# Four buffers instead of two for the sums of overflow rows and of lists in a graph kernel

## The chip, the cores and the metric

One core of one Trainium2 chip. The metric is the device time of one execution in microseconds; the lower the better. The kernel before has a median of 2090.91 us over three runs.

## The reference, cut to what matters

One layer of a graph network: 6250 nodes of 128 features, 200000 edges. Each edge takes the transformed features of its `dst` node, multiplies them by a filter made from 20 edge features, and the products are added up by the edge's `src` node.

```python
h = relu(layernorm(x))                                   # 6250 x 128
xw = h @ W_in
W = (softplus(edge_attr @ W_f1 + b_f1) - log 2) @ W_f2 + b_f2   # 200000 x 128
W = W * edge_weight
m = xw[dst] * W                                          # gather by dst (sorted)
out = segment_sum(m, src, 6250)                          # scatter-add by src (random)
return x + (softplus(out @ W_o1 + b_o1) - log 2) @ W_o2 + b_o2
```

The edges are sorted by `dst`, so a gather reads from a narrow window of rows. The `src` indices are in random order: the segment sum is the costly part.

## The kernel before, in words

The edges are cut into quads of 512 (four chunks of 128); there are 391. A hand-written software pipeline runs one loop iteration `i` per quad. In each iteration the matmuls of several quads at different stages are issued, and at named points (`"D0"`, `"A0"`, `"DM"`, `"PE2"`, `"A2"`, `"D2"`, `"S"` and so on) the loop runs whatever functions were hooked there for this iteration. The order of instructions on each engine is the order of these calls; nothing is rescheduled.

The common part of each quad: PE makes the filter's first product `z` (L313); ACT takes exp and ln of it (tile `a`, L318 and L323); PE gathers node rows by a one-hot matmul (`xg`, L497) and makes the filter `W` (L494, L505); ACT scales the gathered rows into `xc` (L510, four instructions); DVE multiplies `W` by `xc` (L520). PSUM is split into two tags of four banks: "A" (`z`, `xg`, `W`) and "B" (nearly everything else, among it `osum`, `lsum`, `un`, `pq`, `po`).

What becomes of the messages depends on the quad:

- Plain quads (the first and last ones): duplicates within a chunk are summed by a matmul, ACT copies the sums to a tile `s` and makes the indices `ji` (L563), and four scatters follow.
- List quads (192 of them, 768 scatters): the messages in tile `s` are scattered straight from L520's result, with indices prepared ahead (`lji`). Rows that occur twice in a chunk go to a side list in memory; each of 12 such lists is later loaded, summed by a matmul (`lsum`, L469 and L470) and scattered.
- Sorted quads (168 of them): the messages are split into three bf16 parts (tile `pt`, L676, with an extension copied by ACT at L682), permuted into groups of node ranges by matmuls (`pq`, L687), copied to `mst` by ACT (L693), and every eight quads summed straight into node columns by 96 matmuls of a unit (`un`, L781), which DVE adds into `accT` (L792). A unit needs all four "B" banks. Rows that find no slot overflow: they go through `po` (L702 to L704) into `mo` (L710), and every two quads the overflow rows are summed over equal nodes (`osum`, L741) and scattered.

Every scatter is an indirect DMA with accumulation that POOL issues (L582), into one of four accumulators in memory. There are 987: 768 from lists' quads, 123 from plain quads, 96 of the sums of overflow rows and lists (84 + 12).

The part that the change touches is the end of the last two branches. For a pair of sorted quads, or a list, in this order:

1. PE makes the sum in a "B" bank (`over_sum`, or `l_sum`), hooked at `"PE2"`.
2. In the next iteration, at `"A0"`, ACT copies it to the SBUF tile `os` (`over_copy` L746, `l_copy` L475). This frees the PSUM bank. Both write the same tag "os".
3. At `"DM"`, after the iteration's four `xc`, DVE computes the row that the sum goes to (`over_ji` L751, `l_ji` L481, tile `ojd`, three buffers).
4. At `"A2"` ACT turns it into an integer (`over_int` L755, tile `oji`, two buffers).
5. One iteration later, at `"S"`, POOL scatters `os` by `oji` (`over_scatter`).

A tile's buffers are reused in turn. The write to a buffer waits until the instruction that last read it is done; for `os` and `oji` this is the scatter, and "done" means that its data have landed in memory. ACT's instructions run in the order of issue, so a waiting one holds up all behind it. ACT's order in an iteration is: exp and ln of the quad, copies of plain quads, `"A0"` (among it L746, L475, the `mst` and `mo` copies), `ji`, `"A1"`, the four `xc`, then `"A2"` (L755, then L682).

```python
for c in range(4):
    nc.tensor.matmul(W[:, c, :], st[q]["a"][:, c * P:(c + 1) * P], w2, start=False, stop=(c == 3))
...
at(k, "PE2", over_sum, q)
at(k + 1, "A0", over_copy, q)
at(k + 1, "DM", over_ji, q)
at(k + 1, "A2", over_int, q)
at(k + 2, "S", over_scatter, q)
```

After the last scatter the accumulators are loaded, added, transposed and sent through the closing two matrices (L1362 to L1409).

Of the kernel before, what the change touches and what calls it, by code (L numbers as in the profile page):

```python
# [7 lines left out]
F32 = mybir.dt.float32  # L8
# [12 lines left out]
P = 128  # L21
# [33 lines left out]
def tile_gnn(ctx: ExitStack, tc: tile.TileContext, x, fB, cT, srcT, srcr, dstr, win_, wf1, wf2, bias, bo1c, wo1,  # L55
# [53 lines left out]
    sp_ = edge.enter_context(tc.tile_pool(name="sp", bufs=4))  # L109
# [361 lines left out]
        mp["L", j]["sum"] = t  # L471

    def l_copy(j):
        s = sp_.tile([P, 132], F32, tag="os", name="os", bufs=2)
        nc.scalar.copy(s[:, :P + 1], mp["L", j].pop("sum")[:, :P + 1])  # L475
        mp["L", j]["os"] = s

# [264 lines left out]
        mp[q]["sum"] = t  # L742

    def over_copy(q):
        s = sp_.tile([P, 132], F32, tag="os", name="os", bufs=2)
        nc.scalar.copy(s[:, :P + 4], mp[q].pop("sum")[:, :P + 4])  # L746
        mp[q]["os"] = s

# [87 lines left out]
    with tc.manual_schedule():  # L836
# [289 lines left out]
        for w in range((LE - LB) // SW):  # L1126
# [26 lines left out]
            at(k - 1, "L", l_load, w)  # L1153
            at(k, "PE2", l_sum, w)
            at(k + 1, "A0", l_copy, w)
            at(k + 1, "DM", l_ji, w)
            at(k + 1, "A2", over_int, ("L", w))
# [5 lines left out]
        for q in mpq:  # L1163
# [19 lines left out]
            if mpi[q] % 2 or q == mpq[-1]:  # L1183
                at(q + 5, "DM", over_idx, q)
                at(q + 6, "A0", over_dg, q)
                k = clear(q + 6, units)
                at(k, "PE2", over_row, q)
                at(k + 1, "D0", over_eq, q)
                k = clear(q + 8, units)
# [5 lines that stand above are left out]
# [85 lines left out]
    with tc.For_i(0, trips, 1) as ci:  # L1280
# [55 lines left out]
        s = wk.tile([P, P], F32, bufs=1, tag="dg", name="fs")  # L1336
# [259 lines left out]
```

## Time and profile before

| what | us |
|---|---|
| median of three runs (2089.85 to 2092.94) | 2090.91 |
| the profiled execution | 2069.4 |
| its span | 2067.6 |
| PE busy | 1854.7 |
| DVE busy | 1657.1 |
| POOL busy | 1631.5 |
| ACT busy | 1490.1 |

How to read the lines that follow: an engine's row in a timeline begins with the start and the duration in us, then engine, line, operation, output and inputs; in square brackets stands how long the engine was idle just before and what released it. In a view of waits a row says who waited for whom, the sum in us, how many times, and the longest one. In a row of groups, "x768 | 1237.3, 1611 | 266.9" is the count, busy us, mean ns of one, and the idle time just before them. POOL's span of a scatter ends when it has issued it; the data land later.

### The profile page before, as it was taken

The numbers are of one execution on the slowest core, as the hardware profiler recorded it, in microseconds if no ns is written. First come the engines' busy times: TensorE is split into PE (matmuls) and PEld (weight loads), VectorE is DVE, ScalarE is ACT, GpSimd is POOL, SyncE is SP. The second block draws the span as 40 slices with busy tenths as digits, with TensorE's granted clock in tenths as the row PEclk, the third lists the DMA queues.
The fourth block names the chain that finished last, engine by engine and source line by source line (L and its number), as shares of the span: only waits on it lengthen the run. The fifth ranks groups of instructions, "written<-read, shape, count | busy, mean of one in ns | idle before, by whom it ended". The sixth has DMA issues, their size and how long they took to land. (4 is left out here: it accounts for less than half of the span.)

```text
span 2067.6 us, 57535 instructions
## 1 busy us (share of the span) xinstructions
PE 1854.7 (90%) x20381; PEld 1285.7 (62%) x20381; DVE 1657.1 (80%) x4448; ACT 1490.1 (72%) x4083; POOL 1631.5 (79%) x1040
## 2 busy tenths in 40 slices
PE   3489997999999999999999999999999999999956
PEld 2356664666666666666666666666666666677734
DVE  3578896898987888988988978979889787787735
ACT  3368775777776788777778777777778678888714
POOL 3578888888877788887878878888888888888774
PEclk9689998999999999999999999999999999999978
DMA  7887766767766776766667666676676676667648
GB/s 240 227 211 150 125 124 109 128 112 135 130 124 106 126 133 117 136 124 122 121 133 123 122 123 117 118 129 107 129 128 116 112 126 111 110 120 131 129 46 242
DMA packets 381187, 272.56 MB, mean 132 GB/s; under 512 B 97727, under 2 KB 341354, under 8 KB 380898
## 3 DMA queue, kind: packets, MB, share of 16 engines
q0 software_dynamic: 143728, 71.30, 34.9%
q1 hardware_dynamic: 236882, 197.50, 33.8%
q8 instruction: 161, 2.64, 0.5%
q14 instruction: 128, 1.05, 0.2%
q10 hardware_dynamic: 288, 0.07, 0.0%
HBM read 154.45 MB, written 114.24 MB: 130 GB/s over the span
## 5 line engine op out<-in xcount | busy, mean ns | idle before, releaser
L582 POOL DMA_INDIRECT acc<-s,lji x768 | 1237.3, 1611 | 266.9 <-issue 184.6
L687 PE MATMUL pq<-pt,pm 128*128 128x387 bf16 x2688 | 527.9, 339 | 27.0 <-DVE pt L676 10.7
L510 ACT ACTIVATE xc<-xg,cb 128x128 f32<-128x128 f32 x1564 | 446.4, 371 | 121.0 <-PE xg L497 113.8
L505 PE MATMUL W<-w,a 128*128 128x128 f32 x3128 | 464.1, 293 | 0.0
L505 PEld LDWEIGHTS W<-w,a 128*128 128x128 f32 x3128 | 388.7, 196 | 42.0 <-issue 2.6
L781 PE MATMUL un<-so,mst 32*128 32x392 bf16 x8064 | 378.3, 331 | 31.9 <-ACT os L746 19.3
L693 ACT CAST mst<-pq 128x387 bf16<-128x387 f32 x672 | 303.1, 481 | 132.6 <-PE pq L687 130.0
L687 PEld LDWEIGHTS <-pm 128*128 128x128 bf16 x2688 | 259.4, 99 | 211.4 <-issue 16.7
L781 PEld LDWEIGHTS <-mst 32*128 32x128 bf16 x8064 | 228.4, 94 | 175.0 <-issue 70.0
L323 ACT ACTIVATE a<-a,con 128x512 f32<-128x512 f32 x391 | 282.3, 722 | 12.7
L582 POOL DMA_INDIRECT acc<-s,ji x123 | 197.0, 1602 | 82.8 <-issue 25.9
L318 ACT ACTIVATE a<-z 128x512 f32<-128x512 f32 x391 | 237.4, 607 | 33.2 <-PE z L313 17.4
L676 DVE TENSOR_TENSOR pt<-pt 128x512 f32<-128x512 f32 x336 | 231.8, 690 | 5.8
L662 DVE TENSOR_SCALAR pm<-iot,pos 128x576 bf16<-128x576 f16 x672 | 221.4, 390 | 0.0
L520 DVE TENSOR_TENSOR s<-W,xc 128x512 f32<-128x512 f32 x192 | 131.9, 687 | 92.9 <-ACT xc L510 86.0
L792 DVE TENSOR_TENSOR accT<-un,accT 128x392 f32<-128x392 f32 x320 | 158.5, 558 | 58.4 <-PE un L781 58.2
L766 DVE TENSOR_SCALAR so<-iot,mst 128x392 bf16<-128x392 f16 x672 | 191.2, 344 | 5.5 <-PE un L781 5.4
L582 POOL DMA_INDIRECT acc<-os,oji x96 | 155.6, 1621 | 31.1 <-issue 16.2
L497 PE MATMUL xg<-wn,oh 63*128 63x128 bf16 x1564 | 157.2, 222 | 14.5 <-ACT xc L510 8.1
L313 PE MATMUL z<-ft,ws 123*128 123x512 bf16 x391 | 151.6, 388 | 16.1 <-POOL b2rep L927 9.3
L494 PE MATMUL W<-b2rep,onesb 64*128 64x512 bf16 x391 | 153.8, 393 | 0.0
L520 DVE TENSOR_TENSOR pt<-W,xc 128x512 f32<-128x512 f32 x168 | 115.2, 686 | 34.9 <-ACT xc L510 29.4
(209 smaller groups left out, 2431.1 us busy)
## 6 DMA issues: line engine op xcount, KB each, us to landing
rb<-reld SPq DMA_DIRECT2D x391, 64.0 KB
fsd<-f SPq DMA_DIRECT2D x49, 480.0 KB
ft<-fsd SPq DMA_DIRECT2D x195, 120.0 KB
sb<-src SPq DMA_DIRECT2D x169, 128.0 KB
fb<-in_fB_dram SPq DMA_DIRECT2D x49, 320.0 KB
ft<-fsd SPq DMA_DIRECT2D x195, 80.0 KB
wn<-tab SPq DMA_DIRECT2D x782, 15.8 KB
acc<-s,lji POOLq DMA_INDIRECT x768
```

The source lines that it names most:

```text
L318: nc.scalar.activation(a, st[q]["z"], AF.Exp)
L323: nc.scalar.activation(a, a, AF.Ln, bias=half, scale=0.5)
L505: nc.tensor.matmul(W[:, c, :], st[q]["a"][:, c * P:(c + 1) * P], w2, start=False, stop=(c == 3))
L510: nc.scalar.mul(xc[:, c, :], st[q]["xg"][:, c, :], late["c", q // CQ][:, 4 * (q % CQ) + c:4 * (q % CQ) + c + 1])
L520: nc.vector.tensor_tensor(m[:, :, :P], st[q]["W"], st[q]["xc"], op=ALU.mult)
L582: nc.gpsimd.indirect_dma_start(out=accs[k][:rows, :], out_offset=bass.IndirectOffsetOnAxis(ap=ji, axis=0), in_=s, in_offset=None, compute_ ...
L662: nc.vector.tensor_scalar(pm[:, c], iot[:, :SLOTS], rk[r]["pos"][:, 4 * j + c:4 * j + c + 1], None, op0=ALU.is_equal)
L676: nc.vector.tensor_tensor(pt[:, :, k * P:(k + 1) * P], a, high(a), op=ALU.subtract)
L687: nc.tensor.matmul(t[:, :PW], mp[q]["pm"][:, c, s * P:(s + 1) * P], high(mp[q]["pt"][:, c:c + 1, :PW])[:, 0], start=(c == 0), stop=(c == 3))
L693: nc.scalar.copy(mp[q]["ms", s][:, :PW], mp[q].pop(("q", s))[:, :PW])
L766: nc.vector.tensor_scalar(so, iotw[:, :GN], w[:, 3 * P // 2:3 * P // 2 + 1], None, op0=ALU.is_equal)
L781: nc.tensor.matmul(ts[g][:, :GN], mp[q]["ms", s][v, k * P:(k + 1) * P], mp[q]["oh"][v], start=(q == qs[0] and k == 0), stop=(q == qs[-1] a ...
```

## The change

The tag "os" gets four buffers instead of two, at both places that write it. Nothing else is edited; `oji` keeps two buffers and `ojd` three. Each `os` buffer is 132 float32 per partition.

```diff
     def l_copy(j):
-        s = sp_.tile([P, 132], F32, tag="os", name="os", bufs=2)
+        s = sp_.tile([P, 132], F32, tag="os", name="os", bufs=4)
         nc.scalar.copy(s[:, :P + 1], mp["L", j].pop("sum")[:, :P + 1])
...
     def over_copy(q):
-        s = sp_.tile([P, 132], F32, tag="os", name="os", bufs=2)
+        s = sp_.tile([P, 132], F32, tag="os", name="os", bufs=4)
         nc.scalar.copy(s[:, :P + 4], mp[q].pop("sum")[:, :P + 4])
         mp[q]["os"] = s
```

## The prediction

> **What bounds the kernel now.** I read the page first (the parts on busy time, slices, chain of waits and costliest groups), then the views of the tile os, of its two source lines, of the waits of POOL by window, and the timelines of ACT, PE and POOL around the places that these gave.
>
> ```profile
> span 2067.6 us, 57535 instructions
> ...
> PE 1854.7 (90%) x20381; PEld 1285.7 (62%) x20381; DVE 1657.1 (80%) x4448; ACT 1490.1 (72%) x4083; POOL 1631.5 (79%) x1040
> ...
> POOL 3578888888877788887878878888888888888774
> ...
> PE 33%; DVE 7%; ACT 3%; DMA 2%; POOL 2%; issue 1%; SPq 1%; DVEq 0%; POOLq 0%; ACTq 0%
> ...
> L582 POOL DMA_INDIRECT acc<-s,lji x768 | 1237.3, 1611 | 266.9 <-issue 184.6
> ```
>
> Two engines are nearly full. PE is busy 90% and leads the chain of waits. POOL looks free at 79%, but its scatters stand 0.30 us apart even where nothing is waited for (the "issue" rows below), so one scatter occupies about 1.61 + 0.30 = 1.91 us, and the 987 of them (768 + 123 + 96) 1885 us of the 2067.6. The kernel ends with POOL: its last scatters run without a gap, and the closing sums wait for the last one.
>
> ```profile
> 1954.26 1.54 POOL L582 DMA_INDIRECT acc<-s,ji  x1 [2.43 <-ACT ji L563]
> ...
> 2006.32 1.54 POOL L582 DMA_INDIRECT acc<-os,oji  x1 [0.30 <-issue]
> ```
>
> So a gain anywhere counts only if it makes POOL's last scatter earlier, that is, if it removes a POOL pause longer than 0.30 us. Those pauses, from the first stall named below to the second, and from the second to the last scatter:
>
> ```profile
> POOL acc L582 <- issue: 148.5, 487, 0.3
> POOL acc L582 <- DVE s L520: 24.4, 18, 3.0
> ...
> POOL acc L582 <- DVE bn L186: 10.9, 7, 2.2
> ```
>
> ```profile
> POOL acc L582 <- ACT ji L563: 5.8, 5, 2.4
> ...
> POOL acc L582 <- ACT a L318: 1.6, 3, 1.0
> POOL acc L582 <- DMA acc<-os,oji: 1.4, 1, 1.4
> ```
>
> Less 0.30 for each, the first stretch has 24.4 - 5.4 + 10.9 - 2.1 = 27.8 us in which POOL had caught up with the engines that feed it; the second has 4.3 + 0.7 = 5.0 us of that kind, and 1.1 us more that a DMA caused.
>
> **What the change touches.** The view of the tile os:
>
> ```profile
> L582 POOL DMA_INDIRECT acc<-os,oji x96: 1541/1542/2527, 185.5 to 2006.3; - x96
> L746 ACT COPY os<-osum x84: 247/248/269, 154.1 to 1981.2; 128x132 f32<-128x132 f32 x84
> ...
> L475 ACT COPY os<-lsum x12: 247/249/270, 337.7 to 1885.1; 128x129 f32<-128x129 f32 x12
> ...
>   DMA acc<-os,oji: 18.2, 2
> ...
>   PE un L781: 19.3, 4
> ```
>
> With two buffers, copy k must wait until the scatter of copy k-2 has landed. Of the 93 copies that carry such a wait (below), two had to stand: 18.2 us together. In both, PE's unit matmuls (un, L781) stood still behind the copy for the PSUM bank it empties.
>
> **The change part by part.** No instruction is added, dropped or reordered on any engine in the listing of both programs; only ACT's waits differ. All 81 + 12 = 93 DMA waits leave L746 and L475, and 93 appear at L755, the oji write, which keeps its two buffers and whose buffer is read by the same scatter k-2. So the wait isn't removed: it moves down ACT's queue, past the os copy, any mst and mo copies (L693, L710) and the four xc (L510) of the same iteration. Behind it still stand the next pt (L682) and the next exp and ln (L318, L323). SP and POOL are passed by nothing; DMA issues are untouched.
>
> First place, the copy held up near 350 us (ACT, then PE, then the scatter that it waited for on POOL):
>
> ```profile
> 361.25 0.27 ACT L746 COPY os<-osum 128x132 f32<-128x132 f32 x1 [13.77 <-DMA acc<-os,oji]
> ...
> 362.42 0.32 ACT L755 ACTIVATE oji<-ojd,con 128x1 int32<-128x1 f32 x1
> ...
> 368.53 1.14 ACT L510 ACTIVATE xc<-xg,cb 128x128 f32<-128x128 f32 x4 [3.97 <-PE xg L497]
> ```
>
> ```profile
> 361.56 6.58 PE L781 MATMUL un<-so,mst 32*128 32x392 bf16 x93 [14.18 <-ACT os L746]
> ...
> 368.08 0.39 PE L497 MATMUL xg<-wn,oh 63*128 63x128 bf16 x4
> ```
>
> ```profile
> 357.94 1.54 POOL L582 DMA_INDIRECT acc<-os,oji  x1 [0.30 <-issue]
> ```
>
> After the change the copy runs at 361.25 - 13.77 = 347.5, then xc; ACT stands at L755 instead, until the same 361.25. PE does its un (and the next W and xg) inside that wait. From 361.25 on ACT runs the work that began at 362.42, so 1.17 us earlier: it reached the end of it at 368.53 - 3.97 = 364.56, now at 363.4, and there xg is ready. The next xc starts at 363.4 instead of 368.53: a lead of 5.1 us for what feeds POOL. Bounds: nothing (if PE is late anyway) and 13.8 (the whole wait). I take 5.1, since its rows are read directly.
>
> One row speaks against it: after 14 us of idling the 93 un took 6.58 us, where others take 4.09 for 96 (the chain of waits), so 3.96 for 93: a slow restart that costs 2.6 us.
>
> ```profile
> 1657.25 4.09 PE un L781 x96
> ```
>
> The Trainium skill (TensorE: Matmul & The Clock Gate, What's actually happening) says the PE clock falls to half after an idle window of about 3.4 us and returns after as much work. By that rule PE, which would still idle some 7 us ahead of 361.3, restarts slow after the change as well; if PE rather than ACT then decides, the first lead is 2.6 us less and the sum 2064.1 us instead of 2061.5.
>
> The sum stays with 5.1: ACT's own work between 361.3 and 363.4 covers most of a slow restart of PE, and the lead of PE is larger than that of ACT (its pq and xg have no un ahead of them).
>
> Second place (ACT, PE, POOL):
>
> ```profile
> 1633.71 0.27 ACT L746 COPY os<-osum 128x132 f32<-128x132 f32 x1 [4.43 <-DMA acc<-os,oji]
> ...
> 1635.51 0.32 ACT L755 ACTIVATE oji<-ojd,con 128x1 int32<-128x1 f32 x1
> ...
> 1637.87 0.73 ACT L280 CAST f<-fr 128x640 bf16<-128x640 f32 x1 [0.70 <-DVE fr L276]
> 1641.34 1.14 ACT L510 ACTIVATE xc<-xg,cb 128x128 f32<-128x128 f32 x4 [2.75 <-PE xg L497]
> ```
>
> ```profile
> 1634.03 6.92 PE L781 MATMUL un<-so,mst 32*128 32x392 bf16 x93 [4.52 <-ACT os L746]
> ```
>
> Here un fits wholly into the wait: from 1629.5 at the other units' rate it ends at 1633.5, and PE never idles. ACT goes on at 1633.71 with what began at 1635.51 (1.80 earlier), reaches L280 at 1637.17 - 1.80 = 1635.4, and xc at about 1636.0 instead of 1641.34: 5.3 us.
>
> What becomes of each lead? While POOL is behind, it can't use it; it gets it back at the next pauses. The first lead meets 27.8 us of pauses, so it arrives in full. The second meets only 5.0 us, all near the end. On the way it makes POOL later relative to ACT, so a copy with a small margin may now wait. The smallest margin behind 1634 us:
>
> ```profile
> 1756.57 1.54 POOL L582 DMA_INDIRECT acc<-os,oji  x1 [0.30 <-issue]
> ```
>
> ```profile
> 1761.74 0.25 ACT L746 COPY os<-osum 128x132 f32<-128x132 f32 x1
> ...
> 1762.89 0.32 ACT L755 ACTIVATE oji<-ojd,con 128x1 int32<-128x1 f32 x1
> ```
>
> ```profile
> 1762.04 4.14 PE un L781 x93
> ```
>
> The scatter ends at 1758.11 and, by the two stalls (361.25 - 359.48 and 1633.71 - 1631.13), lands 1.8 to 2.6 us later. L755 comes 2.2 to 3.0 us after that. With ACT 5.3 us earlier it would wait 2.3 to 3.1 us. Un's 4.14 us run meanwhile and hide it; without that cover the second lead loses it. Bounds of the second lead at the end: 0 and 5.0. I take 3.5.
>
> Cost of the wait itself. An instruction that waits for two engines gets a separate semaphore instruction:
>
> ```profile
> L746 ACTq EVENT_SEMAPHORE  x41: 17/17/17, 192.5 to 1951.4; - x41
> ...
> L475 ACTq EVENT_SEMAPHORE  x9: 17/17/17, 337.1 to 1750.3; - x9
> ```
>
> ```profile
>   DVE ojd L751: 43.0, 36
> ```
>
> Before there were 50, 17 ns each; now all 93 oji writes wait for DMA and DVE and need one, so 43 more: 0.7 us. The Trainium skill says the same of such instructions (Perfetto Trace Analysis, Identifying Dependency Chains: instructions waiting on several engines may have EventSemaphore instructions inserted ahead of them). ACT is idle 28% of the span, so this is an upper end; nothing is the lower. The larger os tile only shifts addresses in SBUF, at no cost.
>
> Sum: 2069.4 (the profiled execution: 2067.6 of span and 1.8 around it) - 5.1 - 3.5 + 0.7 = 2061.5 us, a ratio of 0.9962. The runs shown have a median of 2090.91, 21.5 us above the profiled execution; nothing in the trace shows why. On their scale the ratio gives 2083 us.
>
> **The rivals.** (A) The wait only changes its place. ACT stands at L755 as long as at L746, everything of the next iteration is behind it, and POOL's own load decides. For it: the DMA that ends the wait is the same, and POOL paces the stretch from 1634 us to the end. Against it: un's work moves ahead of the wait, and POOL has 27.8 us of pauses later. Time: from nothing to one shrunken lead, 5.1 - 2.6 = 2.5 us; 2088.4 to 2091.
>
> (B) Slower: the waits at L755 break ACT's pipelining. Where L755 didn't wait for DVE (93 - 36 = 57 places) it starts ahead of the end of the last xc, as the two timelines show (361.41 + 1.15 against 362.42 at the first place: 0.14 us). If the separate semaphore instruction ends this overlap at the 57 and ACT decides there, that is 57 x 0.14 = 8.0, with the 0.7 some 8.7 us; with the leads lost as in A, about 2099.6 us. It decides once its price exceeds the leads that arrive. Against it: L746 has carried such instructions 41 times and is not seen to start later than without; ACT has idle time in nearly every iteration.
>
> ```profile
> 361.41 1.15 ACT L510 ACTIVATE xc<-xg,cb 128x128 f32<-128x128 f32 x4
> ```
>
> (C) More gain. Margins at several list copies are small, and unprofiled executions are 21.5 us longer; if part of that is further stalls of this kind, twice the forecast's gain, 2 x 7.9, is there: 2075 us. Nothing in the one trace shows it.
>
> **How the numbers follow.** Forecast (both leads arrive in the main) 0.49; A 0.31; B 0.13; C 0.07. 0.2% is 4.2 us, about what a measurement of this kernel can tell from no change. Faster: forecast and C, 0.56; within: A, 0.31; slower: B, 0.13. The predicted time is the forecast's 2083. The range reaches down to C (2075, and 2 us of run spread: 2073) and up past all of A to 2094, which leaves most of B out.
>
> **What would show it.** Right: no idle time ahead of L746 and L475 by DMA; one wait of 12 to 13 us at L755 near 350 us and one of about 2 us near 1632; no un waiting for os; un at about 4.1 us in both places; the next xc some 5 us earlier against the same scatter; POOL's pauses between 362 and 640 us shorter by 5 us in sum. Wrong: POOL's pauses unchanged in sum, new stalls at L755 at other places that stop PE, or L755 starting later after the last xc at most of its places.

## The result, and the profile after

The changed kernel takes 2081.45 us (median of 17 runs) beside 2088.73 us before: a ratio of 0.9967, 95% interval 0.9955 to 0.9979, so some 7 us or 0.33% faster. Two later measurements of the same two kernels, below, gave 0.9966 and 0.9971. The forecast was 0.9962.

The page of the changed kernel's profiled execution:

```profile
span 2077.4 us, 57578 instructions
...
PE 1862.5 (90%) x20381; PEld 1288.0 (62%) x20381; DVE 1659.4 (80%) x4448; ACT 1482.8 (71%) x4083; POOL 1643.9 (79%) x1040
...
PE 31%; DVE 6%; ACT 3%; DMA 3%; issue 2%; POOL 2%; SPq 1%; DVEq 0%; POOLq 0%; ACTq 0%
...
L582 POOL DMA_INDIRECT acc<-s,lji x768 | 1245.7, 1622 | 266.6 <-issue 180.3
```

This one execution is longer than the profiled one of before (2077.4 against 2067.6 us), though the kernel is faster. Single executions of the kernel before lie between 2071 and 2092 us on one chip, so two spans say nothing of a gain of 7 us; that is left to the timed ratios. What a trace does show is where the wait stands and what gets ahead of it. The view of the tile os after the change:

```profile
L582 POOL DMA_INDIRECT acc<-os,oji x96: 1541/1542/2397, 186.8 to 2015.6; - x96
L746 ACT COPY os<-osum x84: 247/248/270, 156.6 to 1991.5; 128x132 f32<-128x132 f32 x84
...
  PE un L781: 2.0, 6
```

The entry "DMA acc<-os,oji: 18.2, 2" is gone from the list of what os waits for, and un waits for os 2.0 us instead of 19.3. The wait itself isn't gone. The view of L755:

```profile
L755 ACT ACTIVATE oji<-ojd,con x96: 294/308/327, 160.3 to 1992.0; 128x1 int32<-128x1 f32 x96
L755 ACTq EVENT_SEMAPHORE  x93: 17/17/17, 197.6 to 1963.1; - x93
...
  DVE ojd L751: 35.3, 27
  DMA acc<-os,oji: 20.0, 3
```

ACT stands 20.0 us at three places, about as long as the 18.2 us before, only further down its queue. The first place, in the timelines of ACT and of PE:

```profile
352.65 0.25 ACT L746 COPY os<-osum 128x132 f32<-128x132 f32 x1
352.80 1.14 ACT L510 ACTIVATE xc<-xg,cb 128x128 f32<-128x128 f32 x4
368.41 0.29 ACT L755 ACTIVATE oji<-ojd,con 128x1 int32<-128x1 f32 x1 [14.47 <-DMA acc<-os,oji]
...
370.28 1.12 ACT L510 ACTIVATE xc<-xg,cb 128x128 f32<-128x128 f32 x4
```

```profile
352.95 4.13 PE L781 MATMUL un<-so,mst 32*128 32x392 bf16 x93 [0.29 <-ACT os L746]
357.02 0.39 PE L494 MATMUL W<-b2rep,onesb 64*128 64x512 bf16 x1
...
368.85 2.74 PE L687 MATMUL pq<-pt,pm 128*128 128x387 bf16 x8 [10.04 <-ACT pt L682]
```

The copy and xc are done at once, un runs in the wait, and so do the next W and xg. Then PE idles 10 us for pt, which ACT makes behind the wait. Before, the next xc came 368.53 - 361.25 = 7.3 us after the wait ended; now it comes 370.28 - 368.41 = 1.9 us after. That is a lead of 5.4 us, where 5.1 was forecast.

The second place, and the one that had the smallest margin (ACT):

```profile
1646.45 0.29 ACT L755 ACTIVATE oji<-ojd,con 128x1 int32<-128x1 f32 x1 [2.81 <-DMA acc<-os,oji]
...
1648.60 1.13 ACT L510 ACTIVATE xc<-xg,cb 128x128 f32<-128x128 f32 x4
```

```profile
1774.06 0.29 ACT L755 ACTIVATE oji<-ojd,con 128x1 int32<-128x1 f32 x1 [2.70 <-DMA acc<-os,oji]
```

At the second, the next xc follows the end of the wait by 2.2 us instead of 1641.34 - 1633.71 = 7.6: 5.4 us. At the third a new wait of 2.70 us appears, where 2.3 to 3.1 was worked out.

### The profile page after: what moved, and what is told of

It reads as the page before. It is cut to its first block, busy times and chain, and to the rows that moved or that the text cites. A ratio compares the mean times of both kernels' runs of the same rounds, so it can differ in the third digit from the quotient of the medians.

```text
span 2077.4 us, 57578 instructions
## 1 busy us (share of the span) xinstructions
PE 1862.5 (90%) x20381; PEld 1288.0 (62%) x20381; DVE 1659.4 (80%) x4448; ACT 1482.8 (71%) x4083; POOL 1643.9 (79%) x1040
## 5 line engine op out<-in xcount | busy, mean ns | idle before, releaser
L323 ACT ACTIVATE a<-a,con 128x512 f32<-128x512 f32 x391 | 282.3, 722 | 12.7
L582 POOL DMA_INDIRECT acc<-s,ji x123 | 200.2, 1628 | 80.4 <-issue 26.4
L318 ACT ACTIVATE a<-z 128x512 f32<-128x512 f32 x391 | 238.3, 610 | 26.8 <-PE z L313 17.2
L520 DVE TENSOR_TENSOR s<-W,xc 128x512 f32<-128x512 f32 x192 | 131.9, 687 | 85.9 <-ACT xc L510 52.0
L520 DVE TENSOR_TENSOR pt<-W,xc 128x512 f32<-128x512 f32 x168 | 115.2, 686 | 47.9 <-ACT xc L510 29.5
```

The lines of the kernel that those rows point to most:

```text
L318: nc.scalar.activation(a, st[q]["z"], AF.Exp)
L323: nc.scalar.activation(a, a, AF.Ln, bias=half, scale=0.5)
L520: nc.vector.tensor_tensor(m[:, :, :P], st[q]["W"], st[q]["xc"], op=ALU.mult)
L582: nc.gpsimd.indirect_dma_start(out=accs[k][:rows, :], out_offset=bass.IndirectOffsetOnAxis(ap=ji, axis=0), in_=s, in_offset=None, compute_ ...
```

## The experiments

All ratios are to the kernel before, timed on the same chip beside each run. A ratio compares all runs and can differ by 0.1% from the quotient of the two medians. The rows stand for 12 runs each, those from both deeper to lists apart for 6, the last one for 2. The chips differ by more than the change brings: the kernel before has medians of 2071.1, 2082.5 and 2082.9 us on the three chips of these runs. The lead theory says: the gain is the work of ACT and PE that gets ahead of the wait. Its rivals: the move alone does nothing and POOL's load decides; or any change of buffers does this.

| kernel | os / oji buffers | median us, before us | ratio, 95% interval |
|---|---|---|---|
| before, again | 2 / 2 | 2082.7, 2082.5 | 1.0006, 0.9987 to 1.0026 |
| before, a third time | 2 / 2 | 2084.3, 2082.9 | 1.0006, 0.9990 to 1.0022 |
| only oji deeper | 2 / 4 | 2082.5, 2082.5 | 1.0006, 0.9990 to 1.0022 |
| oji write later | 2 / 2 | 2071.0, 2071.1 | 1.0007, 0.9990 to 1.0023 |
| changed, again | 4 / 2 | 2073.4, 2082.5 | 0.9966, 0.9950 to 0.9983 |
| changed, a third time | 4 / 2 | 2076.2, 2082.9 | 0.9971, 0.9955 to 0.9987 |
| changed, oji write later | 4 / 2 | 2063.9, 2071.1 | 0.9965, 0.9947 to 0.9984 |
| both deeper | 4 / 4 | 2060.4, 2082.5 | 0.9904, 0.9883 to 0.9925 |
| both three | 3 / 3 | 2063.3, 2082.9 | 0.9910, 0.9888 to 0.9932 |
| both four, oji write later | 4 / 4 | 2063.7, 2082.9 | 0.9911, 0.9893 to 0.9928 |
| lists apart | 2 + 2 / 2 + 2 | 2051.3, 2071.1 | 0.9912, 0.9889 to 0.9934 |
| no scatter of sums | 4 / 2 | 2040.0, 2071.1 | 0.9857, 0.9819 to 0.9895 |

**The two kernels again.**

> The kernel before once more, on the chip of the next three. All theories: a ratio of 1.000 within 0.002. Lead theory (what counts is how much of ACT's and PE's work gets ahead of the wait): again a wait of 12 to 15 us ahead of L746 near 350 us with un (L781) idle for as long, and the next xc (L510) 7 to 8 us after the wait ends.

> The changed kernel once more. Lead theory: a ratio of 0.9955 to 0.998; the wait of 12 to 15 us now ahead of L755, the next xc about 2 us after it ends, un idle for under 3 us in sum because of os. Rival (only the place of the wait changes, POOL's load decides): the same wait, but a ratio within 0.002 of 1.

> The kernel before a third time, for one more trace and timing on this chip: ratio 0.998 to 1.002; a wait of 12 to 15 us ahead of L746 near 350 us and one of 1 to 5 us near 1640 us.

> The changed kernel a third time: ratio 0.995 to 0.998. Counted from the iteration ahead of the first stall, the tenth iteration behind it starts 4 to 5 us sooner than in the kernel before; single executions scatter by more than that at the end.

All four came as the lead theory has it: 12.6 and 13.7 us ahead of L746 in the traces of the kernel before, 12.1 and 12.7 us ahead of L755 in those of the changed one. Two sizes were a little off: in the first repeat of the kernel before the next xc comes 6.5 us after the wait, not 7 to 8, and in the last pair the 67th iteration of the table below starts 5.5 us sooner, not 4 to 5 (4.7 as the mean over all traces). Only the second, small stall is unsteady: 1.8 and 4.4 us before, none at that place in these two after. The rival that puts the ratio within 0.002 of 1 falls.

**Only oji deeper.**

```diff
-        ji = sp_.tile([P, 1], I32, tag="oji", name="oji", bufs=2)
+        ji = sp_.tile([P, 1], I32, tag="oji", name="oji", bufs=4)
```

> os keeps two buffers, oji gets four. Lead theory: the wait stays ahead of L746, no work gets ahead of it, so a ratio of 0.998 to 1.002. Rival (any change of buffers or of their places in SBUF moves the time as the change did): about 0.9967.

1.0006. In its view of os the wait is still there:

```profile
  PE un L781: 19.1, 7
  ACT os L746: 17.4, 2
```

(the list of who waited: un for os, and the copy itself for the scatter that reads os). So it isn't more buffers of any kind, or other places of them, that bring the gain.

**Both deeper.** The changed kernel with the same edit of oji.

> Four buffers for os and for oji, so the wait is gone and not only moved. Lead theory: at the first place ACT gains the whole 13.8 us instead of some 5.4, and POOL has 27.8 us of later pauses to take it in: 6 to 9 us below the changed kernel, a ratio to before of 0.992 to 0.994. Rival (POOL's backlog decides: with the wait gone the tile s, which has four buffers, holds DVE up instead): the same ratio as the changed kernel, 0.996 to 0.998, with new waits of 5 us and more at L520 on scatters.

0.9904: 20 us below before and 13 below the changed kernel, clear of the rival's bounds, and more than the 6 to 9 us expected of the lead theory, which had counted the first place alone. The whole of the two waits came back (18.2 us in the profile of before; 12.6 + 1.8 to 13.7 + 4.4 in the repeats). ACT at the first place:

```profile
351.43 0.25 ACT L746 COPY os<-osum 128x132 f32<-128x132 f32 x1
351.58 1.14 ACT L510 ACTIVATE xc<-xg,cb 128x128 f32<-128x128 f32 x4
352.59 0.32 ACT L755 ACTIVATE oji<-ojd,con 128x1 int32<-128x1 f32 x1
...
356.72 1.14 ACT L510 ACTIVATE xc<-xg,cb 128x128 f32<-128x128 f32 x4 [1.99 <-PE xg L497]
```

No wait at either line; the next xc comes 5.3 us after the copy, where it took 17.6 in the changed kernel. The granted TensorE clock stays at 1.00 from 340 to 380 us, so that PE's slow restart is gone as well. The tile s did not take the wait over: L520 waits for scatters 1.9 us in all.

**Lists apart.** os and oji keep two buffers; the sums of lists get tags of their own, two buffers each.

```diff
     def l_copy(j):
-        s = sp_.tile([P, 132], F32, tag="os", name="os", bufs=2)
+        s = sp_.tile([P, 132], F32, tag="los", name="os", bufs=2)
...
     def over_int(q):
-        ji = sp_.tile([P, 1], I32, tag="oji", name="oji", bufs=2)
+        t_ = "loji" if isinstance(q, tuple) else "oji"
+        ji = sp_.tile([P, 1], I32, tag=t_, name="oji", bufs=2)
```

> os and oji keep two buffers for overflow sums, and the lists' sums get two of their own for each. Lead theory, with the stalls put down to the lists (a list's sum between two overflow sums takes a buffer out of turn): an overflow copy then waits for a scatter one turn earlier, no wait is left at L746, L475 or L755, and the ratio is that of four buffers for both, 0.988 to 0.993. Rival (two buffers are too few whatever the lists do): waits of 5 us and more stay and the ratio is 0.995 to 1.001.

0.9912 and no wait at any of the three lines. This names the cause of the stalls. Overflow copies come some 20 us apart, a scatter waits its turn on POOL for up to 35 us, and two buffers just suffice, until a list's sum comes in between and takes one. At both stalls of the kernel before the order was overflow sum, list, overflow sum, and the third had to wait for the first's scatter. The copies ahead of the first stall and of the second:

```profile
322.81 0.25 ACT L746 COPY os<-osum 128x132 f32<-128x132 f32 x1
...
337.69 0.25 ACT L475 COPY os<-lsum 128x129 f32<-128x129 f32 x1
```

```profile
1605.64 0.25 ACT L746 COPY os<-osum 128x132 f32<-128x132 f32 x1
...
1616.16 0.27 ACT L475 COPY os<-lsum 128x129 f32<-128x129 f32 x1 [0.29 <-PE lsum L470]
```

Behind the first place DVE now waits a little for s instead:

```profile
DVE s L520 <- DMA acc<-s,lji: 8.0, 4, 3.0
```

**Both three.**

> Three buffers for os and for oji. In the traces of before, the scatter three back had ended 14 us ahead of the copy at the first stall, so three are enough: no wait at L746, L475 or L755, ratio as with four of each, 0.988 to 0.993. Rival (depth itself brings more): between the changed kernel and four of each, 0.993 to 0.997.

0.9910 and no wait at the three lines: three are enough, as the scatter three back was always done.

**The oji write one iteration later.** In the changed kernel, in the one before, and with four buffers for both:

```diff
-            at(k + 1, "A2", over_int, ("L", w))
+            at(k + 2, "A2", over_int, ("L", w))
...
-                at(k + 1, "A2", over_int, q)
+                at(k + 2, "A2", over_int, q)
```

> The changed kernel (os four, oji two) with the oji write one iteration later, still ahead of its scatter. Lead theory: pt, exp, ln and the next four xc get ahead of the wait too, about 3 to 5 us of ACT's work more than in the changed kernel, so 3 to 6 us below it: a ratio to before of 0.993 to 0.9955. Rival (moving a wait that isn't removed brings a fixed amount, whatever stands ahead of it): 0.996 to 0.998 as the changed kernel.

> The kernel before (two buffers for both) with the oji write one iteration later. It has what later_os4 does besides moving the wait: ACT no longer idles ahead of L755 for DVE's ojd (about 43 us in sum). Lead theory: that idle time isn't on the path that sets the end, and the wait stays at L746: 0.997 to 1.002. Rival: ACT's idle time ahead of L755 counts, then several us are gained, 0.993 to 0.997.

> Four buffers for both and the oji write one iteration later. Lead theory: no wait is left to be moved, and ACT's idle time for ojd was off the path, so the same as four of each: 0.988 to 0.993. Rival (that idle time counts once the stalls are gone): below 0.988.

The two controls came as the lead theory had them, 1.0007 and 0.9911: ACT's idle time ahead of L755 for DVE's ojd (43.0 us before, none here) was worth nothing. The first missed. 0.9965 is the changed kernel's ratio, not 0.9930 to 0.9955. The trace shows why the expectation was too large:

```profile
352.74 1.14 ACT L510 ACTIVATE xc<-xg,cb 128x128 f32<-128x128 f32 x4 [1.52 <-PE xg L497]
363.62 0.29 ACT L755 ACTIVATE oji<-ojd,con 128x1 int32<-128x1 f32 x1 [9.75 <-DMA acc<-os,oji]
363.82 0.58 ACT L318 ACTIVATE a<-z 128x512 f32<-128x512 f32 x1
```

The second xc does get ahead of the wait, but in the changed kernel all of pt, exp, ln and xc took only 371.28 - 368.41 = 2.9 us after it (the next exp began at 371.28). Counted from the anchor of the table below, the 67th iteration starts at 53.6, 1.4 us sooner than in the changed kernel, less than 0.1%, and the interval is 0.18% wide on each side. The direction agrees with the lead theory; the timing can't tell it from the rival, which stays open.

**No scatter of sums.** The scatter of the 96 sums is left out, the rest of the changed kernel stays.

> The changed kernel without the 96 scatters of overflow and list sums (these sums are left out of the output). If POOL's load sets the end, 96 x 1.91 = 183 us of it are gone and the time falls until PE sets it: over 40 us below the changed kernel. If PE sets the end and POOL has room, it falls by under 20 us.

Between the two: about 23 us below the changed kernel (0.9857 against 0.9966 to 0.9971), and only some 10 below the kernels without the wait, for 183 us less of POOL's work. With two runs either difference is uncertain by some 8 us. POOL's waits in it:

```profile
POOL acc L582 <- issue: 207.1, 676, 0.6
POOL acc L582 <- DVE s L520: 126.9, 51, 7.6
POOL acc L582 <- ACT ji L563: 46.6, 10, 18.7
POOL acc L582 <- DVE bn L186: 34.8, 15, 5.3
```

So most of what is taken from POOL turns into waiting for the engines that feed it. They in turn wait for PE: DVE's `s` for ACT's xc (87.3 us), ACT's xc for PE's xg (105.0 us), and PE is busy 91%. PE's side sets the pace, with POOL close behind.

**The traces laid side by side.** The starts of the exp (L318) of each iteration, read from ACT's timelines and counted from the 58th, the last but two ahead of the first stall:

```
iteration   four traces with the stall at L746     three of the changed kernel   both 4, both 3, both 4 later, apart
67th        59.7  58.5  60.6  60.0                 56.0  54.5  54.5              44.4  44.2  45.2  43.4
319th       1283.3 1292.6 1291.6 1293.6            1288.1 1292.6 1288.4          1281.5 1279.1 1281.4 1265.5
325th       1318.5 1324.1 1325.6 1328.2            1319.9 1322.2 1318.6          1310.1 1307.1 1310.4 1294.3
391st       1627.4 1635.4 1636.6 1640.9            1631.5 1633.2 1629.6          1621.2 1618.2 1622.2 1603.4
```

(The four are the three of the kernel before and the one with only oji deeper; the kernel before with the later oji write, which stalls at L746 too, has 59.3 at the 67th. Lists apart ran on the chip of 2071.1 us, so its later rows don't compare with the others.) At the 67th the groups are well apart: 59.7 on average, 55.0 and 44.3. The first lead is 4.7 us, and 15.4 with the wait gone; that is more than the wait itself (12.6 to 13.8 us), as PE's slow restart behind it is gone too. From the 319th to the 325th, across the second place, the groups take 33.8, 30.5 and 28.6 us: leads of 3.3 and 5.2. At both places together that makes 8.0 us for the changed kernel and 20.6 for the wait-free ones, beside timed gains of some 7 and of 18 to 20 us. In between single executions drift by 10 us, so that no trace follows a lead to the end; only the wait-free kernels remain visibly ahead.

## Why the prediction was right

- **The wait moves, it doesn't go.** Right: 20.0 us in three places at L755, none at L746 and L475; un waits 2.0 instead of 19.3 us. The controls show that it is this: deeper oji alone does nothing, deeper both brings 0.9904. The first wait was to be 12 to 13 us; it is 14.5, 12.1 and 12.7 in the three traces.
- **The first lead, 5.1 us.** 5.4 in the two rows that the forecast named, 4.7 as the mean of the traces.
- **PE's slow restart.** After 10.04 us of idling the eight pq took 2.74 us, where eight take 1.40 in the many rows of the chain of waits of before: 1.3 us of loss, not 2.6, and ACT's exp, ln and xc covered it. One of these rows:

```profile
1088.26 1.40 PE pq L687 x8
```

  The granted TensorE clock shows the restart itself. It is 0.50 from 349.5 to 366.6 us in the kernel before and from 361.3 to 371.6 in the changed one. At the second place it is 0.50 from 1632.9 to 1639.7 before, where un took 6.92 us, and 1.00 after the change: there the slow restart is gone, as the forecast's "PE never idles" had it. By the Trainium skill (TensorE: Matmul & The Clock Gate, What's actually happening) an idle window of about 3.4 us halves the clock until PE has been busy for such a window. The traces agree: the three slow stretches last 17.07, 10.24 and 6.83 us, which is 5, 3 and 2 times 3.41. At the first place un, which no longer idles first, took 4.13 us instead of 6.58.
- **The second lead, 5.3 us, of which 3.5 was to arrive.** 5.4 by the rows of the two profiled executions, 3.3 as the mean over traces, since the wait that it comes from is between 1.8 and 4.4 us. The new wait at the place of the smallest margin was foreseen with its size (2.70 us); in another execution it is 3.7 us, in a third it isn't there.
- **The cost of the semaphore instructions, 0.7 us, and the rival that built on it.** The 93 rows are there at 17 ns; whether they cost any time at the end no run resolves. L755 starts at least 0.1 us ahead of the end of the last xc at 48 of 88 places, before at 49: the overlap isn't lost, and the rival that made the kernel slower falls.
- **POOL as what sets the end.** This is the step that was off. Two of its statements failed. POOL's pauses were to shrink by 5 us between 362 and 640 us; in the profiled execution they didn't. The view of POOL's waits between the first and the second place:

```profile
POOL acc L582 <- issue: 146.5, 480, 0.3
POOL acc L582 <- DVE s L520: 24.9, 12, 4.7
...
POOL acc L582 <- DVE bn L186: 6.8, 6, 2.1
```

  Less 0.30 each that is 24.9 - 3.6 + 6.8 - 1.8 = 26.3 us against 27.8, and between 362 and 640 us alone 6.8 against 6.9: "POOL's pauses unchanged in sum" was one of the forecast's own signs of being wrong. Over all scatters of an execution the pauses beyond 0.305 us sum to 62 to 69 us in the four traces with the stall, to 59 to 65 in the three of the changed kernel and to 33 to 53 in the wait-free ones. The first two groups overlap, and with the later oji write it is 53.8 us with two buffers for os and 53.3 with four. So the traces don't show that the change shortened POOL's pauses; the scatters themselves stretch by amounts that vary more (durations beyond 1.542 us sum to 68 to 80 us from one execution to the next). And POOL isn't nearly full, as the forecast's 1885 us suggested: without 183 us of its work the kernel gained some 10 us over the wait-free one. The leads arrive because PE's side is the slower one and POOL waits for it, which the forecast had only as a condition.
- **The gain of the rivals.** That the wait only changes its place (A) was right about the wait and wrong about the gain. Further stalls in unprofiled runs (C) are not needed: the repeats' traces have the same two.

The sum, a ratio of 0.9962, against 0.9967: the first lead was 4.7 us for 5.1, the second 3.3 us at its place for 5.3, and the 0.7 us isn't resolved. Where the leads come from was right by the rows. That the second is close to the 3.5 us of the sum is luck: the forecast took off 1.8 us for what would be lost on the way, while the wait behind this lead is unsteady. That the leads arrive was right for another reason than the one given, and that the ratio came within 0.0005 is luck in part too, as the interval is 0.0012 wide on each side. The 21.5 us between the profiled execution and the three runs, which the forecast left open, may be a difference of chips; that isn't shown.

## What to carry to other kernels

When one instruction reads two buffers, deepening one only hands the wait to the writer of the other; look through all tiles that the slow reader holds. Even so a moved wait gains what can run ahead of it, here a PSUM bank for PE, and the gain is read from the rows between the old and the new place. When two producers share a tag, count the buffers at the place where both write in a row: three were enough here, or a tag for each.

## What the runs showed of the hardware

The wait-free kernels got back all of the stalled time: 0.9904 to 0.9912, or 18 to 20 us, for 14.4 to 18.2 us of stalls in the traces, though both PE (90%) and POOL (79%, and 0.30 us between any two scatters) looked too full to make up for it. A scatter takes 1.54 us undisturbed, yet 250 to 290 of the 987 take 1.57 us or more, and what they take beyond 1.542 us sums to 68 to 80 us, differently in each execution. That this is why equal programs differ by 1% isn't shown: in the traces of the kernel before the sum and the span rise together (68.0 us with a span of 2067.6, 75.1 with 2079.7, 79.6 with 2082.7), in those of the changed kernel they don't (72.9 with 2078.0, 76.0 with 2073.4, 80.4 with 2077.4). The granted TensorE clock does go with the time: of 29 runs of the kernel before on one chip the shortest, 2071.2 us, had 0.966 and the longest, 2091.8 us, had 0.958 (correlation -0.66). Which of the two causes the other the runs don't show.
